# Background work of a scan kernel regrouped into one beat per unit, with read-outs moved and the positive part rebuilt from |s|/2

## The chip, the cores and the metric

One Trainium2 chip, one of its cores. The metric is device time in microseconds (us) of the one launch. Engines are named as in the profile: PE (TensorE: matmuls; PEld its weight loads), DVE (VectorE), ACT (ScalarE), POOL (GpSimd), SP (SyncE, which here only issues DMAs).

## What is computed

Sixteen images of 64 x 64 x 96 in fp32 pass two residual layers, `x = x + L0(gn(x))` and `x = x + L1(gn(x))`, where `gn` is a group norm over 32 groups. Cut to what matters:

```python
def L0(x):      # upsample by FFT, quadratic activation between two 1x1 products, low-pass, take every second
    h = upsample(x) @ W1.T + b1
    h = coef[:, 0] + coef[:, 1] * h + coef[:, 2] * (h * h)
    return lowpass(h @ W2.T + b2)[::2, ::2]

def L1(x):      # a selective scan in four directions
    xc, z = split(x @ in_proj_w.T)
    z = silu(z)
    xc = silu(conv3x3_depthwise(xc) + conv_b)
    xs = stack([rows(xc), columns(xc), reversed rows, reversed columns])     # K = 4, d = 192, L = 4096
    dts, Bs, Cs = split(xs . x_proj_weight)                                   # 6, 16, 16
    delta = softplus(dts . dt_projs_weight + dt_projs_bias)
    # per k, d and state n of 16, along L:
    h[t] = exp(delta[t] * A[n]) * h[t-1] + delta[t] * xs[t] * Bs[t, n]
    y[t] = sum_n h[t, n] * Cs[t, n]   (+ xs * Ds)
    y = layernorm(sum of the four directions) * z
    return y @ out_proj_w.T
```

## The kernel before

**Order.** The program is written out by hand (`manual_schedule`): each engine runs its instructions in exactly the order of the Python calls, and each waits in order. SP issues all DMAs and waits in order too. So what counts is where a call stands among the others of its engine.

**The loop.** `scan` runs 16 images x 8 steps x 6 blocks x 4 units = 3072 units. A step is 1024 positions of one pair of directions; a block is one of six groups of 64 rows (two halves e of 32, each times 4 states on 128 partitions); a unit (n) is one j of four groups of 4 states. `POS = 3 * 8 * 6 * NQ` is the number of slots of an image, three a unit. Per unit:

- POOL makes `b = dtu * bt` for unit n + 2 (`drive`, L827, 128 x 2048), after the odd half's product with ct of unit n (`odd`, L977) in three units of four.
- ACT makes `da = exp(delta * a)` for unit n + 1, one half at a time (`decay`, L821), into PSUM, one buffer a half; and copies the end state of a half (`keep`, L844).
- DVE runs the odd half's scan (`recur(n, 1)`, L836 forwards or L838 backwards), the even half's, then the even half's product with ct (L988). At j = 3 the odd half's product is on DVE too (L968), between the scans.
- PE sums the products over the states (`read_out`, L861, 16 matmul instructions with `fold_s`), in the block's y, with a start from the stored part (L853) in the second pair. `store` copies y (ACT, L872) and writes it out.

Calls of a unit in order: odd scan, odd decay of n + 1, **slot 0**, (odd product and its keep at j = 3), second half of a pending store, odd product on POOL, drive of n + 2, even scan, DVE's keep, **read_out(n - 1)**, **slot 1**, even product, even keep, even decay of n + 1, store of the last block (if unit n - 1 ended one), **slot 2**, fetches.

**Slots.** A slot advances `block_work` and, if due, the background. `block_work` has twelve slots a block (0 to 11: j times 3 plus the slot). In it `task` makes delta and dtu of 128 x 512 for the next use: at slot 0 s = dtw . pr (PE, L683); 1: |s| and exp(-|s|) (ACT); 2: relu(s) and w = 1 + e; 3: ln(1 + e); 4: 1 - w; 6: the sum w + e + ln + relu by four products with the identity (PE, L699) into a new s; 9: dtu = s * u (DVE, L703); 10: delta = s (ACT, L705) and a DMA; 11: the other DMA. In blocks 2 and 3 `mix` (PE, L661) and, in the next block's slot 0, `mixed` (ACT, L666) prepare the next step. All of s and pp share one PSUM bank.

**The background** of image mi is `front(mi + 1)` and after it `finish(mi - 1)`, Python generators that are spread evenly over the slots: a step is due while `n * positions < at * slices`, with 540 slices for front and 117 for finish. In the loop they have two PSUM banks (`b_ps`, bufs 2) and eleven SBUF pieces (L182). `front` has, in order: loads of xt; `norm` (8 sums L205, 8 squares L218 on ACT); the u/h/o part, 4 passes of 3 u groups (L327, copied out at L338) and 5 groups of widen (L278, L285), three h products (L370) with squares (L351), o (L382, copied at L310) and for each second one d (L294, copied at L361, stored by `stow` L303); the e part (L440, L445, put back at L430); a second `norm`; xgp (L459); and the conv part, 12 tiles of 9 taps and z (L487, L499) with two Silu and two table loads on ACT. A step that yields `WAIT` (before the Silus) is only followed at slot 2 of j = 2. `finish` has, for each of 8 tiles: two centred sums yc (L557, L570, ten instructions each), their squares (ACT, L566, L585), yc * z (DVE, L579, L590), the variance v (L586, L591), Ln and Exp (L596, L597), o (L600), DVE's o * r (L606), and the sum e of ob . z0, ob . z1, ident . x1 (L604) and ident . r (L610), copied and written out one step later. For the first image `front(0)` runs alone ahead of the loop, and for the last one `finish(15)` runs alone after it.

Of the kernel before, what the change touches and what calls it, by code (L numbers as in the profile page):

```python
# [70 lines left out]
POS = 3 * 8 * 6 * NQ  # L71
SLICES = 540
FINISH = 117
WAIT = -1


@with_exitstack
def tile_two_blocks(
# [31 lines left out]

    one_s = const.tile([128, 1], F32, name="one_s")
# [14 lines left out]
    ob_s = const.tile([128, 2, C], F32, name="ob_s")  # L126

    with tc.tile_pool(name="setup", bufs=1) as sp, tc.tile_pool(name="setup_ps", bufs=1, space=PSUM) as spp:
# [45 lines left out]
        for i in range(2):  # L174
            nc.vector.tensor_scalar(pd_s[:, i, :], pmat_s[:, i, :], dsum[:, i:i + 1], None, ALU.mult)
            nc.vector.tensor_scalar(ow_s[:, i, :], op_r[:, i, :], on_r[:, i, 0:1], None, ALU.mult)
            nc.vector.tensor_scalar(ob_s[:, i, :], op_r[:, i, :], on_r[:, i, 1:2], None, ALU.mult)

# [3 lines left out]
    b2p = ctx.enter_context(tc.tile_pool(name="b2", bufs=11))  # L182
# [10 lines left out]
    def parts(out, in_, n=4):  # L193

        step = L // n
        for i in range(n):
            nc.sync.dma_start(out=out[:, step * i:step * i + step], in_=in_[:, step * i:step * i + step])  # L197
            yield

    def norm(xt):  # L200

        s = small.tile([C, 8], F32, name="gs")
        for t in range(8):
            junk = piece([C, TB], "junk")
            nc.scalar.activation(junk, xt[:, TB * t:TB * t + TB], AF.Identity, accum_out=s[:, t:t + 1])  # L205
            if t % 2:
                yield
        yield
# [7 lines left out]
        for t in range(8):  # L216
# [4 lines left out]
            if t % 2:  # L221
                yield
        yield
# [10 lines left out]
        yield  # L234
        yield
        return rg, nb

    def front(mi):
# [8 lines left out]
        yield from parts(xt, xc[mi])  # L247
        yield
# [6 lines left out]
        yield  # L255
        yield
# [3 lines left out]
        yield  # L260
# [51 lines left out]
        o_last = None  # L312
        asked = []
        for p0 in range(0, UPS, PP):

            t1 = b18.tile([HW, PP, C], F32, name="t1", tag="b18")
            if not asked:
                asked += [fetch_x(0), fetch_x(1)]
                for _ in range(3):
                    yield  # L320
            for cg in range(3):
                xr = asked.pop(0)
                u_ps = [bank([HW, 16, PP], "u_ps") for _ in range(2)]
                for k in range(16):
                    for a in range(2):
                        on = slice(64 * a, 64 * a + 64)
                        nc.tensor.matmul(  # L327
                            u_ps[a][:, k, :], lhsT=xr[k // 8][on, k % 8, :], rhs=up_s[on, p0:p0 + PP],
                            start=True, stop=True,
                        )  # L330
                    if k == 7:
                        yield
# [3 lines left out]
                for a in range(2):  # L336
                    c0 = 48 * a + 16 * cg
                    nc.scalar.copy(t1[:, :, c0:c0 + 16], u_ps[a].rearrange("w c p -> w p c"))  # L338
                    yield
# [3 lines left out]
            yield  # L343
            for g in range(PP // PG):
                row = p0 + PG * g
                h_ps, hsq = [None] * HB, [None] * HB
                sd = None

                def square(j):
                    hsq[j] = piece([128, PG * UPS], "hsq")  # L350
                    nc.scalar.activation(hsq[j], h_ps[j], AF.Square, bias=b1_s[:, j:j + 1])  # L351

                for j in range(HB + 1):
                    if j == 0 and o_last is not None:
                        keep_o(o_last)
                    elif j == 1 and len(t2) == 2:
                        square(0)
                        d_ps = narrow()
                        yield
                        sd = piece([128, PG * C], "sd")  # L360
                        nc.scalar.copy(sd, d_ps)  # L361
                    elif j:
                        square(j - 1)
                    if j == 2 and sd is not None:
                        stow(sd, row - 2 * PG)
                    if j >= 2 and g == PP // PG - 1 and p0 + PP < UPS:
                        asked.append(fetch_x(j - 2))
                    if j < HB:
                        h_ps[j] = bank([128, PG * UPS], "h_ps")
                        nc.tensor.matmul(  # L370
                            h_ps[j], lhsT=w1t_s[:, 128 * j:128 * (j + 1)],
                            rhs=xu.rearrange("c p q -> c (p q)"), start=True, stop=True,
                        )
                    elif g < PP // PG - 1:
                        xu_ps = widen(t1, g + 1)
                    yield
                o_ps = bank([UPS, PG, C], "o_ps")
                for p in range(PG):
                    if p == 2:
                        yield  # L380
# [5 lines left out]
                    if p == 1 and g < PP // PG - 1:  # L386
                        xu_next = normed(xu_ps)
                o_last = o_ps
                if g < PP // PG - 1:
                    xu = xu_next  # L390
                yield
            if p0 + PP < UPS:
                keep_o(o_last)
                o_last = None
                yield
                if len(t2) == 2:
                    d_ps = narrow()
                    yield
                    sd = piece([128, PG * C], "sd")
                    nc.scalar.copy(sd, d_ps)  # L400
                    yield
                    stow(sd, row - PG)
        keep_o(o_last)
        yield
        d_ps = narrow()
        yield
        sd = piece([128, PG * C], "sd")
        nc.scalar.copy(sd, d_ps)
        yield
        stow(sd, UPS - 2 * PG)  # L410


        def fetch_s(first, n):
            t = b18.tile([UPS, n, C], F32, name="s", tag="b18")
            for k in range(0, n, 8):
                nc.sync.dma_start(out=t[:, k:k + 8, :], in_=s_d[:, first + k:first + k + 8, :])
                yield t, first

        JS = 40
        for _ in range(2):  # L420
            yield
# [700 lines left out]
```

## Time and profile before

| | us |
|---|---|
| median of 3 runs (20474.57 to 20484.85) | 20479.29 |
| the profiled execution: its own time | 20473.08 |
| its span | 20471.3 |
| first drive on POOL (end of `front(0)` and the first tasks) | 468.9 |
| last product on DVE | 20308 |
| tail, `finish(15)` alone | 163 |
| busy: DVE / POOL / PE / ACT | 19208.3 / 19150.8 / 16699.0 / 13815.5 |

A row of the page's fifth part reads: line, engine, operation, output <- inputs, shape, count | busy us, mean ns of one | idle time of the engine just ahead of these instructions, and what ended most of it. In the timeline the idle time ahead of an instruction and its releaser stand in brackets. Neighbouring instructions of DVE and POOL overlap by some 0.07 us in these records, so a chain of them is read from start to start. The page's span does not hold the 1.8 us around the execution.

### The profile page before, as it was taken

The page shows a single profiled execution, that of the slowest core. Times are in us where ns is not written, and L with a number is a line of the kernel's source. Part 1 is how long each engine was busy: PE and PEld are TensorE (multiplying, and loading weights), DVE is VectorE, ACT ScalarE, POOL GpSimd, SP SyncE. Part 2 cuts the span into 40 slices and gives each one's busy share as a digit, 9 for nine tenths or more (in the row PEclk, how much of TensorE's full clock was granted, in tenths as well). Part 3 has the DMA queues.
Part 4 walks back from the last instruction along what each step waited for, and adds up shares of the span by engine and source line. Part 5 has one row for each costly group of instructions (what it writes and reads, how often), then busy time and mean ns, then how long its engine had stood idle before and what let it go on. Part 6 is the DMA issues. An engine that isn't in the chain of part 4 may idle for free. (4 is left out here: it accounts for less than half of the span.)

```text
span 20471.3 us, 274485 instructions
## 1 busy us (share of the span) xinstructions
PE 16699.0 (82%) x98988; PEld 7171.0 (35%) x98988; DVE 19208.3 (94%) x12989; ACT 13815.5 (67%) x20694; POOL 19150.8 (94%) x5384
## 2 busy tenths in 40 slices
PE   7877888888888878788887888888887787888767
PEld 4423334343333433334233343433334333242222
DVE  0999999999999999999999999999999999999997
ACT  4676767667676776766767676676767767677554
POOL 0999999999999999999999999999999999999996
PEclk8888898988889889888888889888898888888888
DMA  2666666766667676666766667667676666766664
GB/s 85 212 224 208 223 234 211 242 214 222 231 218 239 210 240 220 217 235 214 235 218 221 234 215 238 218 220 234 217 237 210 234 223 216 238 217 232 221 214 157
DMA packets 1966064, 4478.55 MB, mean 219 GB/s; under 512 B 461726, under 2 KB 560958, under 8 KB 1962654
## 3 DMA queue, kind: packets, MB, share of 16 engines
q1 hardware_dynamic: 1964702, 4461.00, 64.5%
q8 instruction: 781, 12.80, 0.3%
q14 instruction: 581, 4.76, 0.1%
HBM read 3581.91 MB, written 878.18 MB: 218 GB/s over the span
## 5 line engine op out<-in xcount | busy, mean ns | idle before, releaser
L827 POOL TENSOR_TENSOR b<-dtu,bt 128x2048 f32<-128x2048 f32 x3072 | 13903.4, 4538 | 471.7 <-DMA dtu<-dtu_d 467.9
L821 ACT ACTIVATE da<-delta,a_s 128x1024 f32<-128x1024 f32 x6144 | 6868.4, 1118 | 2264.3 <-DVE b L988 849.7
L977 POOL TENSOR_TENSOR odd<-b,ct 128x1024 f32<-128x1024 f32 x2304 | 5456.2, 2368 | 679.3 <-DVE b L836 246.2
L988 DVE TENSOR_TENSOR b<-da,ct 128x1024 f32<-128x1024 f32 x3072 | 3760.5, 1224 | 41.8
L836 DVE TENSOR_TENSOR_SCAN da<-da,new,b 128x1024 f32<-128x1024 f32 x1440 | 3372.8, 2342 | 82.6 <-ACT da L821 78.9
L838 DVE TENSOR_TENSOR_SCAN da<-da,new,b 128x1024 f32<-128x1024 f32 x1440 | 3370.2, 2340 | 15.8 <-ACT da L821 14.7
L861 PE MATMUL y<-b,fold_s 128*32 128x256 f32 x30720 | 2561.2, 427 | 797.7 <-ACT yt L872 411.5
L844 ACT COPY new<-da 128x1 f32<-128x1 f32 x2880 | 457.1, 159 | 2434.9 <-DVE b L988 1892.3
L836 DVE TENSOR_TENSOR_SCAN b<-da,new,b 128x1024 f32<-128x1024 f32 x864 | 2023.8, 2342 | 29.3 <-ACT da L821 28.3
L838 DVE TENSOR_TENSOR_SCAN b<-da,new,b 128x1024 f32<-128x1024 f32 x864 | 2022.5, 2341 | 29.2 <-ACT da L821 29.2
L487 PE MATMUL c_ps<-xgp,wtap_s 96*64 96x512 f32 (+1 forms) x4608 | 1764.7, 640 | 77.7 <-ACT row L505 71.9
L861 PEld LDWEIGHTS y<-b,fold_s 128*32 128x32 f32 x30720 | 739.7, 114 | 2919.4 <-issue 1557.0
L861 PE MATMUL y<-odd,fold_s 128*32 128x256 f32 x18432 | 1599.9, 421 | 197.3 <-POOL odd L977 197.0
L683 PE MATMUL s<-pr,dtw_s 128*128 128x512 f32 x1536 | 1034.5, 761 | 689.9 <-ACT delta L705 574.0
L661 PE MATMUL pp<-u,xpt_s 128*128 128x512 f32 x1536 | 891.7, 726 | 461.4 <-ACT delta L705 319.1
L699 PE MATMUL s<-w,ident_s 128*128 128x512 f32 x1534 | 1054.0, 775 | 238.4 <-ACT w L694 211.5
L370 PE MATMUL h_ps<-xu,w1t_s 96*128 96x500 f32 x1920 | 1038.8, 642 | 166.1 <-ACT hsq L351 121.1
L836 DVE TENSOR_TENSOR_SCAN da<-da,b 128x1024 f32<-128x1024 f32 x480 | 1096.2, 2284 | 79.2 <-ACT da L821 75.1
L838 DVE TENSOR_TENSOR_SCAN da<-da,b 128x1024 f32<-128x1024 f32 x480 | 1095.2, 2282 | 10.7 <-ACT da L821 9.2
L382 PE MATMUL o_ps<-w2c_s,hsq 128*100 128x96 f32 x9600 | 1009.2, 263 | 71.6 <-ACT hsq L351 71.3
L382 PEld LDWEIGHTS o_ps<-w2c_s,hsq 128*100 128x100 f32 x9600 | 946.0, 176 | 266.2 <-ACT hsq L351 111.4
L487 PEld LDWEIGHTS c_ps<-xgp,wtap_s 96*64 96x64 f32 (+1 forms) x4608 | 631.8, 177 | 1081.2 <-issue 942.6
(140 smaller groups left out, 23002.7 us busy)
## 6 DMA issues: line engine op xcount, KB each, us to landing
dtu<-dtu_d SPq DMA_DIRECT2D x1536, 512.0 KB
delta<-delta_d SPq DMA_DIRECT2D x1536, 512.0 KB
bt<-rows SPq DMA_DIRECT2D x1024, 512.0 KB
ct<-rows SPq DMA_DIRECT2D x1024, 512.0 KB
u<-xs_d SPq DMA_DIRECT2D x1664, 256.0 KB
dtu_d<-dtu SPq DMA_DIRECT2D x767, 256.0 KB
delta_d<-delta SPq DMA_DIRECT2D x767, 256.0 KB
xr<-in_x SPq DMA_DIRECT2D x768, 128.0 KB
```

Source lines behind the costliest of these rows:

```text
L370: nc.tensor.matmul(h_ps[j], lhsT=w1t_s[:, 128 * j:128 * (j + 1)], rhs=xu.rearrange("c p q -> c (p q)"), start=True, stop=True,)
L382: nc.tensor.matmul(o_ps[:, p, :], lhsT=hsq[j][:, UPS * p:UPS * (p + 1)], rhs=w2c_s[:, j, :], start=(j == 0), stop=(j == HB - 1),)
L487: nc.tensor.matmul(c_ps[p:p + n], lhsT=wtap_s[:, tap, 128 * i:128 * i + n], rhs=xgp[:, h0:h0 + 8, dx:dx + HW], start=(tap == 0), stop=(tap ...
L683: nc.tensor.matmul(s, lhsT=dtw_s[:, pair, v, :], rhs=ctx["pr"][t], start=True, stop=True)
L699: nc.tensor.matmul(s, lhsT=ident_s, rhs=of, start=(i == 0), stop=(i == 3))
L821: nc.scalar.activation(da, deltas[n // NQ, e], AF.Exp, scale=a_s[:, k, g, units[n][2]:units[n][2] + 1])
L827: nc.gpsimd.tensor_mul(b, dtus[n // NQ], bt.unsqueeze(1).to_broadcast([128, 2, T]))
L836: nc.vector.tensor_tensor_scan(out, da, b, before, ALU.mult, ALU.add)
L838: nc.vector.tensor_tensor_scan(out[:, ::-1], da[:, ::-1], b[:, ::-1], before, ALU.mult, ALU.add)
L861: nc.tensor.matmul(y[32 * q:32 * q + 32, e, :], lhsT=fold_s, rhs=weighed[e][:, QT * q:QT * q + QT], start=(pair == 0 and j == 0 and e == 0 ...
L977: nc.gpsimd.tensor_mul(odds[n], h, bc[1, r, j])
L988: nc.vector.tensor_mul(bs[n][:, 0, :], h, bc[1, r, j])
```

## The change

It moves and regroups the background; some instructions go.

- **Beats.** The even spread (`POS`, `SLICES`, `FINISH`, `due`) goes. A background advances once per unit, at slot 2; a step that ended in `LIGHT` is also followed at slot 1 and once more at slot 2; one that ended in `VEC` is followed at slot 0 only; `WAIT` stays. front has 176 steps and finish 66 (383 and 114 before); in images 1 to 14 front ends in the image's unit 147 (149 before) and finish in 188 (189 before).
- **Banks.** In `front`, a beat first copies out what the last beat's products left in the two banks (`empty`, the squares, `normed`), then issues new products. `parts` issues its DMAs at once, `stow` and the write of out stand right behind their copies.
- **finish** has per tile, in beats: centre; at slot 0 `rooted` (DVE's o * r and e of the last tile) and loads, at slot 2 square and the last tile's copy out; at slot 0 yz0 and the second centre, at slot 2 its square; at slot 0 yz1 and v, at slot 2 Ln, Exp and o. Every second tile is followed by an empty beat. e is three products, not four: z1 and x1 share one tile zx, x1's last 32 rows stand below r in rx.
- **norm** of the second layer takes its sums from the puts of the e part (`accum_out`), with two tiles in flight.
- **task** starts at slot 11 of the block before; |s| and exp at slot 1, w at 2, ln, 1 - w and the four products at 4, dtu and delta at 9, both DMAs at 10. dtw is halved at the start; s holds s/2, and |s|/2 (`half_s`) is added in the same bank, so Relu and the second s go. mix is at slot 10 and mixed at 11 of the same block.
- **read_out(n)** stands after the even decay of unit n, ahead of slot 2; the store of a block stands in the next unit after the even scan, ahead of slot 1.
- b2 has 12 pieces.

```diff
-    def norm(xt):
+    def norm(xt, s=None):
...
-        s = small.tile([C, 8], F32, name="gs")
-        for t in range(8):
-            junk = piece([C, TB], "junk")
-            nc.scalar.activation(junk, xt[:, TB * t:TB * t + TB], AF.Identity, accum_out=s[:, t:t + 1])
-            if t % 2:
-                yield
-        yield
+        if s is None:
+            s = small.tile([C, 8], F32, name="gs")
+            for t in range(8):
+                junk = piece([C, TB], "junk")
+                nc.scalar.activation(junk, xt[:, TB * t:TB * t + TB], AF.Identity, accum_out=s[:, t:t + 1])
+                if t < 7:
+                    yield LIGHT
...
+        def empty(p0):
+            nonlocal u_ps, o_ps, d_ps
+            if u_ps is not None:
+                for cg, ps in u_ps:
+                    for a in range(2):
+                        c0 = 48 * a + 16 * cg
+                        nc.scalar.copy(t1[:, :, c0:c0 + 16], ps[a].rearrange("w c p -> w p c"))
+            if o_ps is not None:
+                t2.append(piece([UPS, PG, C], "t2"))
+                nc.scalar.copy(t2[-1], o_ps)
+            if d_ps is not None:
+                sd = piece([128, PG * C], "sd")
+                nc.scalar.copy(sd, d_ps)
+                stow(sd, rows.pop(0))
+            u_ps = o_ps = d_ps = None
...
+                empty(p0)
+                grow(0)
+                grow(1)
+                yield
+                square(0)
+                square(1)
+                grow(2)
+                if more:
+                    xu_ps = widen(t1, g + 1)
...
+                yield
+                square(2)
+                if more:
+                    xu = normed(xu_ps)
                 o_ps = bank([UPS, PG, C], "o_ps")
...
+        def rooted(o_ps, r, z0, zx, rx):
+            nc.vector.tensor_mul(rx[0:C], o_ps, r)
+            e_ps = bank([C, TB], "oe_ps")
+            for i, (w, of) in enumerate(((ob_s[:, 0, :], z0), (ob_s[:, 1, :], zx), (ro_s, rx))):
+                nc.tensor.matmul(e_ps, lhsT=w, rhs=of, start=(i == 0), stop=(i == 2))
+            return e_ps
...
+        for t in range(9):
+            yc0 = centre(t, 0, 128) if t < 8 else None
+            yield VEC
+            if left is not None:
+                e_ps = rooted(*left)
...
+                yield
+                sq0 = squared(yc0, 128)
...
+            yield VEC
+            yz0 = scaled(yc0, z0, 128)
+            yc1 = centre(t, 1, 64)
+            yield
+            sq1 = squared(yc1, 64)
+            yield VEC
+            yz1 = scaled(yc1, zx[0:64], 64)
...
-                nc.scalar.activation(m, s, AF.Relu)
...
+                nc.scalar.activation(m, s, AF.Abs, scale=2.0)
+                nc.scalar.activation(e, m, AF.Exp, scale=-1.0)
+                yield
                 nc.scalar.activation(w, e, AF.Identity, bias=one_s)
                 yield
+                yield
                 nc.scalar.activation(d, e, AF.Ln, bias=one_s)
-                yield
                 nc.scalar.activation(w, w, AF.Identity, scale=-1.0, bias=one_s)
-                yield
-                yield
-                s = ps.tile([128, TB], F32, name="s", tag="g")
-                for i, of in enumerate((w, e, d, m)):
-                    nc.tensor.matmul(s, lhsT=ident_s, rhs=of, start=(i == 0), stop=(i == 3))
-                for _ in range(3 - late):
+                for by, of in ((half_s, m), (ident_s, w), (ident_s, e), (ident_s, d)):
+                    nc.tensor.matmul(s, lhsT=by, rhs=of, start=False, stop=(of is d), skip_group_check=True)
+                for _ in range(5):
                     yield
                 dtu, delta = make("dtu"), make("delta")
                 nc.vector.tensor_mul(dtu, s, u)
-                yield
                 nc.scalar.copy(delta, s)
...
+                def at(self, position):
+                    if self.gen is None:
+                        return
+                    if position == 2:
+                        if self.said == LIGHT:
+                            self.step()
+                        if self.gen is not None and self.said != VEC and (self.said != WAIT or j == NQ - 2):
+                            self.step()
+                    elif self.said == (VEC, LIGHT)[position]:
+                        self.step()
...
-                if n >= 1:
-                    read_out(n - 1)
+                if n >= 1 and j == 0:
+                    storing = store(n - 1)
+                    next(storing)
                 slot(1)
...
                 if n < last:
                     decay(n + 1, 0)
-                if n >= 1 and units[n - 1][2] == NQ - 1:
-                    storing = store(n - 1)
-                    next(storing)
+                read_out(n)
                 slot(2)
```

## The prediction

> **What bounds it.** I read the page's first part, then its costliest groups, then the waits of DVE and POOL inside the loop, then the busy time by step of one image, and last a stretch of the timeline. The page:
>
> ```profile
> span 20471.3 us, 274485 instructions
> PE 16699.0 (82%) x98988; PEld 7171.0 (35%) x98988; DVE 19208.3 (94%) x12989; ACT 13815.5 (67%) x20694; POOL 19150.8 (94%) x5384
> ...
> L827 POOL TENSOR_TENSOR b<-dtu,bt 128x2048 f32<-128x2048 f32 x3072 | 13903.4, 4538 | 471.7 <-DMA dtu<-dtu_d 467.9
> ...
> L977 POOL TENSOR_TENSOR odd<-b,ct 128x1024 f32<-128x1024 f32 x2304 | 5456.2, 2368 | 679.3 <-DVE b L836 246.2
> L988 DVE TENSOR_TENSOR b<-da,ct 128x1024 f32<-128x1024 f32 x3072 | 3760.5, 1224 | 41.8
> ```
>
> Two engines are full. POOL has no work for 468 us (the first image's front), and then all but stands still nowhere. Four units (one block) cost POOL four drives, 4.49 us from start to start in the timeline at 10000, and three odd products, 2.31: 24.9 us. DVE in a block, by the same timeline: three units of 5.77 (two scans, 2.26 and 2.24; a copy, 0.13; a product, 1.14) and one of 7.5 with a second product and the dtu product: 24.8. So neither hides the other, and the loop's length is DVE's work plus DVE's idle time. By step, with one image in the middle (image 7) cut at the first scan of each step (columns: length, PE, PEld, DVE, ACT, POOL busy, clock, DMA):
>
> ```profile
> 9466.00:9628.00 162.00, 137.73 (x1028) 75.54 (x1027) 149.62 (x104) 112.27 (x177) 148.83 (x43) 0.86 0.58 195
> 9628.00:9780.30 152.30, 111.14 (x696) 53.22 (x694) 148.66 (x90) 107.08 (x162) 150.43 (x43) 0.82 0.65 222
> ...
> 10083.30:10245.70 162.40, 138.71 (x587) 46.60 (x587) 154.37 (x112) 99.56 (x149) 151.89 (x43) 0.89 0.80 265
> ...
> 19107.80:20300.70 1192.90, 793.53 (x3925) 267.10 (x3924) 1187.67 (x798) 687.11 (x979) 1186.39 (x335) 0.78 0.59 206
> ```
>
> Steps count from 0. DVE and POOL each need 147 to 152 us per step (154 in step 6, which has products of finish on DVE). The lengths differ, up to 162: that is waiting. The last image, with no front behind it, takes 1192.9 / 8 = 149.1 a step. This is the floor. What DVE waits for inside the loop (us, times, longest):
>
> ```profile
> DVE dtu L703 <- PE s L699: 285.7, 224, 3.8
> DVE da L836 <- ACT da L821: 154.0, 149, 3.5
> DVE b L838 <- ACT da L821: 88.2, 73, 2.4
> DVE b L836 <- ACT da L821: 36.5, 45, 1.4
> DVE da L838 <- ACT da L821: 23.9, 47, 0.6
> ```
>
> That is 285.7 for the step sums and 302.6 for decays, 588 of 20471 us: the whole prize inside the loop. One place shows how both come about:
>
> ```profile
> 9479.22 4.07 PE L382 MATMUL o_ps<-w2c_s,hsq 128*100 128x96 f32 x30
> ...
> 9483.12 1.05 PE L699 MATMUL s<-w,ident_s 128*128 128x512 f32 x2
> ...
> 9486.78 0.69 DVE L703 TENSOR_TENSOR dtu<-s,u 128x512 f32<-128x512 f32 x1 [0.80 <-PE s L699]
> ...
> 9487.62 0.68 ACT L351 ACTIVATE hsq<-h_ps,b_s 128x500 f32<-128x500 f32 x1 [3.74 <-PE h_ps L370]
> ...
> 9489.54 2.36 DVE L836 TENSOR_TENSOR_SCAN da<-da,new,b 128x1024 f32<-128x1024 f32 x1 [0.93 <-ACT da L821]
> ```
>
> The four ident products stand behind the background's 30 products on PE; dtu waits 0.80 us. A background square on ACT waits 3.74 us for its bank; the decay behind it is late and the scan waits 0.93.
>
> **Step sums.** Now the ident products are issued at slot 6 of a block's twelve, dtu at slot 9. After: slot 4 and 9, in the same bank, with half|s| added in place of a Relu. So PE has five slots, some 10 us, for 3.6 us of products (9483.12 to 9486.7) and at most one background lump ahead (o_ps 3.2 and d_ps 1.3). Laid out from the end of a block's first scan: DVE takes dtu at 17.3; ACT has w at about 9.9; the sum ends at 12.5 to 15. I take all 285.7 away (bounds -220 to -285.7, the lower if a lump is late now and then). What is late next is POOL, at 24.9 a block. The Relu, 0.59 x 768 = 450 us of ACT, is not on the path, but gives room to decays.
>
> **Decays.** A scan of the even half starts 2.26 us after the even product ends; in that time ACT must copy the end state (0.16, 0.25 after the product) and make the decay (1.12): 0.7 us to spare. The odd decay has 2.4 to spare. The change moves all evacuation behind the even decay, where the spare is the odd decay's. Heaviest usual beat: square and normed, 0.67 + 0.76; the slack holds, with 0.3 us left at slot 4, where Ln and w (1.43) come ahead of the even decay. Where it does not hold: the LIGHT beats (sums, squares, xgp), three a unit, each 0.71 + 0.19. ACT then has per block 9.0 of decays, 0.8 of copies, 4.0 of task, 0.6 of yt and 10.8 of background, 25.2, and in awkward order. They fill some 18 units an image. Today's waits in these places (steps 0 and 4) are about 6.7 us an image, and I leave them. Of the other 200 us half goes: -100 (bounds -250 to +100).
>
> **Banks.** Only two background banks exist in the loop, and a refill now always follows its evacuation in the same beat. In the list of waits PE stands 110.0 us before u_ps and 121.1 before h_ps for ACT to empty a bank; both will grow, by up to 1 us in each of some 150 beats of 15 images, 2200 us of PE. I charge nothing. PE's products in a u/h/o block are some 10.5 us of lumps (u 2.8, h 1.1 each, xu 1.3, o 3.2 and d 1.3 by the rows of the loop), 4 of read-outs, 4.3 of task and 0.9 of mix, 20 out of 24.8, so it has the room; and a lump that starts at 5.8 and lasts 4.4 ends before ACT returns for it at 11.2. If that cover is gone, each lost us comes out as a late bank, then as a late decay (bounds 0 to +230: 0.5 us in each of 31 u/h/o and conv blocks of 15 images). The Trainium skill (Perfetto Trace Analysis, Matmuls) speaks against the change here: groups should rotate through banks, so that one's evacuation overlaps the next one's products; by it the sum would be up to 2200 us higher if PE were the end, and by the rows, where PE waits and nothing waits for it, it stays as it is.
>
> **Read-outs** go half a unit forward on PE, right behind the even product, and the block's store with them. POOL waits behind PE for its odd buffers now (y 68.9, pp 57.4, s 29.3 us), and PE waits for yt (411 and 341 us, by the list of waits). Both shrink, but DVE hardly waits for b (5.4 us), so 0.
>
> **Finish** runs in 42 units before and after (66 beats against 114 slices). But its products for DVE now stand directly behind the odd scan, and each waits for ACT's square, itself behind PE. Take the tile whose centre starts at j=0, from that block's first scan: read-out 3.5 to 4.5, centre 4.5 to 9.0, e_ps 2.6 to 11.6, ident products 8 x 0.43 to 15.0, read-out 16.0, second centre to 20.5, square to 21.1; DVE wants yz1 at 17.9. That is 3.2 us of wait. From j=1, 2 and 3 I get 2.0, 0.3 and 1.3. Two tiles of each: 13.6 us an image; the decays' and squares' shares that are hidden by drift bring it to 10. Fifteen images: +150 (bounds 0 to +400: no wait at all, or one half of a unit per tile). No like wait is in the trace within the loop (0.6 us), so this is the least certain term.
>
> **Ends.** The last image's finish is spread over 188 units now; afterwards it stands in 42, with its waits: +15 (0 to +30). The first front loses the second norm's eight sums (8 x 0.81 us), but two puts come late: -5. The tail's eight tiles each lose two PE products of 0.43: -7. SP now issues xt, x1, ycol in one go; ycol is 3 MB, and in the tail the same took 11.5 us to land, while the next dtu has 14. On SP stow and out now stand directly behind the copies that they store, so SP waits for ACT's beat, and behind it stand the fetches of dtu, delta, bt and ct; these are asked for 11 us or more ahead of use, and SP waits 5134 us for dtu today without harm: 0 for both (to +40).
>
> Sum: -286 - 100 + 150 + 15 - 12 = -233. The profiled execution took 20473.1 (its span and 1.8), 6 us under the median of the runs: 20473 - 233 = **20240 us**, -1.2%.
>
> **Rivals.** (a) Forecast, 20080 to 20420: 0.48. (b) The waits really go: DVE's drop by 500 and finish stays hidden: 20473 - 286 - 230 + 30 = about 19990. For it: blocks in the conv stretch already run at 24.8 with a beat-like order. 0.24. (c) The change only trades waits, within 0.2% (what a measurement of this kernel can tell from no change, some 41 us): finish's waits at about 3 us a tile. 0.08. (d) Slower: the same mechanism beyond its turning point. 120 tiles share out 286 + 100 + 12 - 15 = 383 us, so from 3.2 us of wait per tile on average the change loses. If centre, e_ps and ident products stand in line for a whole unit, 6.2 us a tile, it costs 744: 20830. PE, in order and 95% busy in the last step of this image (149.1 of 157.5), speaks for it; that finish has only 10 of 48 blocks, and that the products are asked a unit apart, speaks against. 0.20.
>
> The range, 19950 to 20620, leaves out the ends of (b) and the worse half of (d). Faster 0.72, same 0.08, slower 0.20.
>
> **What would show it.** DVE's wait for s under 20 us in the loop; decay waits 150 to 250, most of them in steps 0 and 4; steps 1 to 3 at 150 to 152 us each; new waits of yz for sq, about 150 us in all, the largest where the tile starts at j=0; POOL's wait for PE almost gone; a front of some 464 us and a tail of 156. Wrong it is if DVE's wait for decays grows in steps 1 to 3 (the slack at slot 4 is gone), or if yz waits exceed 400.

## The result, and the profile after

The changed kernel takes 20817.57 us (median of 4 runs, 20800.98 to 20818.47), the kernel before 20482.07 beside it: 1.0162 times as long [1.0145, 1.0180]. The forecast was 20240, with a range up to 20620. Its rival (d) named the sign, a wait in finish; that is one of two causes, and the smaller one.

The page of the profiled execution after (20818.47 us, span 20816.7), with the rows that answer to those of before and the row of the product on y0 (the stored part of y, with which a block's read-out begins in the second pair of directions):

```profile
span 20816.7 us, 273741 instructions
...
PE 16622.4 (80%) x98732; PEld 7192.1 (35%) x98732; DVE 19213.7 (92%) x12996; ACT 13446.3 (65%) x19798; POOL 19141.3 (92%) x5384
...
L824 POOL TENSOR_TENSOR b<-dtu,bt 128x2048 f32<-128x2048 f32 x3072 | 13894.7, 4534 | 466.3 <-DMA dtu<-dtu_d 454.7
...
L975 POOL TENSOR_TENSOR odd<-b,ct 128x1024 f32<-128x1024 f32 x2304 | 5438.7, 2361 | 1049.8 <-DVE b L835 562.5
...
L850 PE MATMUL y<-y,ident_s 128*128 128x512 f32 x768 | 550.1, 806 | 752.3 <-DMA y<-part 589.4
```

DVE and POOL do the same work in the same time as before (19213.7 and 19141.3 us busy, 19208.3 and 19150.8 before). The 345 us between the two profiled executions are idle time, but for 5 us of DVE. Image 7 by steps (2, 3, 4, 6 and the last image; columns as before):

```profile
9591.00:9742.70 151.70, 128.88 (x1096) 70.49 (x1096) 148.69 (x103) 104.52 (x164) 149.94 (x43) 0.86 0.67 228
9742.70:9895.40 152.70, 121.69 (x830) 65.62 (x830) 148.16 (x85) 101.32 (x142) 152.45 (x43) 0.90 0.60 205
9895.40:10059.40 164.00, 126.14 (x669) 43.35 (x670) 147.29 (x108) 116.54 (x172) 149.72 (x42) 0.87 0.66 222
...
10214.60:10396.00 181.40, 145.98 (x614) 50.42 (x614) 155.86 (x114) 98.97 (x145) 152.23 (x43) 0.89 0.74 245
...
19435.70:20655.70 1220.00, 787.02 (x3914) 257.99 (x3918) 1190.49 (x798) 674.86 (x935) 1184.83 (x335) 0.78 0.58 201
```

Step 2 fell from 162.0 to 151.7; steps 4 and 6 rose (4 to 7 are the second pair of directions), step 6 from 162.4 to 181.4. Over images 1 to 14, us a block by step, from the starts of the odd scans (the lower rows are runs told below):

| step | 0 | 1 | 2 | 3 | 4 | 5 | 6 | 7 | last image |
|---|---|---|---|---|---|---|---|---|---|
| before | 25.98 | 25.55 | 26.52 | 25.35 | 25.32 | 25.18 | 27.13 | 26.25 | 24.98 |
| after | 25.06 | 24.92 | 25.24 | 25.49 | 27.44 | 25.84 | 30.19 | 27.18 | 25.55 |
| read-outs alone | 25.72 | 26.12 | 25.87 | 25.92 | 25.93 | 26.38 | 27.67 | 27.05 | 25.38 |
| task alone | 25.27 | 25.63 | 25.87 | 25.27 | 25.24 | 24.96 | 26.70 | 26.59 | 24.96 |
| y0 ahead of the beat | 25.10 | 24.91 | 25.13 | 25.49 | 25.49 | 25.07 | 29.11 | 27.00 | 25.52 |
| late first centre | 25.06 | 24.90 | 25.13 | 25.55 | 25.73 | 25.01 | 26.54 | 26.92 | 24.97 |

A difference of 1 in a step is 84 us (14 images, six blocks). Steps 0 to 3 together won 2.69 x 84 = 226 us, steps 4 to 7 lost 6.77 x 84 = 569, the last image 0.57 x 48 = 27: 370 for the loop. Front and tail won 13.2 and 9.6 (first drive at 455.7 us, tail 153.8). With 2 us less for the loop of image 0, which the table leaves out, that is the 345 us. What DVE and PE wait for in the loop after (us, times, longest):

```profile
DVE b L835 <- ACT new L841: 263.4, 101, 9.2
DVE yz L556 <- ACT sq L551: 258.2, 95, 4.7
DVE da L833 <- ACT da L818: 120.4, 68, 4.8
DVE yz L556 <- DMA z<-z_d: 101.5, 26, 6.7
DVE dtu L694 <- PE s L690: 94.7, 59, 4.1
DVE da L835 <- ACT da L818: 70.9, 76, 3.7
```

```profile
PE y L858 <- DVE b L987: 2251.0, 990, 13.3
PE y L850 <- DMA y<-part: 589.4, 165, 9.2
...
PE h_ps L363 <- ACT hsq L370: 94.5, 76, 1.5
...
PE u_ps L345 <- ACT t L326: 38.4, 16, 5.2
```

Three of DVE's waits are new (under 5 us each before): the end state `new` from ACT, the square, and z0. On PE, the wait for y0 was not there before. One place at the end of step 4 shows what it does. The DMA queue first, then PE, ACT and DVE in the timeline:

```profile
10022.48 0.34 SPq L697 DMA_DIRECT2D dtu_d<-dtu  x1
10028.02 0.34 SPq L698 DMA_DIRECT2D delta_d<-delta  x1
...
10031.69 5.81 SPq L512 DMA_DIRECT2D xs_d<-col  x8
10037.60 0.63 SPq L763 DMA_DIRECT2D y<-part  x1
```

```profile
10040.60 2.05 PE L850 MATMUL y<-y,ident_s 128*128 128x512 f32 x2 [7.93 <-DMA y<-part]
...
10051.76 0.69 DVE L694 TENSOR_TENSOR dtu<-s,u 128x512 f32<-128x512 f32 x1 [3.22 <-PE s L690]
...
10052.66 1.99 PE L484 MATMUL c_ps<-xgp,wtap_s 96*128 96x512 f32 x4
...
10054.68 0.69 ACT L500 ACTIVATE row<-c_ps,convb_s 128x512 f32<-128x512 f32 x1 [5.69 <-PE c_ps L484]
...
10057.45 0.59 ACT L695 COPY delta<-s 128x512 f32<-128x512 f32 x1
10057.93 0.17 ACT L841 COPY new<-da 128x1 f32<-128x1 f32 x1
10058.13 1.12 ACT L818 ACTIVATE da<-delta,a_s 128x1024 f32<-128x1024 f32 x1
10059.18 0.15 ACT L841 COPY new<-da 128x1 f32<-128x1 f32 x1
10059.35 2.35 DVE L835 TENSOR_TENSOR_SCAN b<-da,new,b 128x1024 f32<-128x1024 f32 x1 [2.30 <-ACT new L841]
```

The fetch of y0 stands behind eight stores of col on SP, 5.81 us of issuing. PE, which needs y0 half a unit earlier than before, stands 7.93 us. Behind y0 on PE stand the taps of the convolution and the ident products of s: DVE's dtu waits 3.22 us for s, ACT waits 5.69 us for the last taps in a Silu, and behind the Silu stand delta, two end states and the decays. The scan waits 2.30 us.

### The profile page after: what moved, and what is told of

Its sections match the earlier page's. It is cut to its first block, busy times and chain, and to the rows that moved or that the text cites. A ratio compares the mean times of both kernels' runs of the same rounds, so it can differ in the third digit from the quotient of the medians.

```text
span 20816.7 us, 273741 instructions
## 1 busy us (share of the span) xinstructions
PE 16622.4 (80%) x98732; PEld 7192.1 (35%) x98732; DVE 19213.7 (92%) x12996; ACT 13446.3 (65%) x19798; POOL 19141.3 (92%) x5384
## 5 line engine op out<-in xcount | busy, mean ns | idle before, releaser
L858 PE MATMUL y<-b,fold_s 128*32 128x256 f32 x30720 | 2640.4, 439 | 2272.0 <-DVE b L987 2254.9
L835 DVE TENSOR_TENSOR_SCAN da<-da,new,b 128x1024 f32<-128x1024 f32 x1440 | 3371.7, 2341 | 2.7 <-ACT da L818 1.7
L835 DVE TENSOR_TENSOR_SCAN b<-da,new,b 128x1024 f32<-128x1024 f32 x864 | 2023.4, 2342 | 188.4 <-ACT new L841 187.4
L484 PE MATMUL c_ps<-xgp,wtap_s 96*64 96x512 f32 (+1 forms) x4608 | 1688.5, 623 | 5.5 <-ACT xgp L454 5.5
L675 PE MATMUL s<-pr,dtw_s 128*128 128x512 f32 x1536 | 1146.2, 837 | 70.1 <-ACT pr L660 69.9
L835 DVE TENSOR_TENSOR_SCAN da<-da,b 128x1024 f32<-128x1024 f32 x480 | 1095.8, 2283 | 71.5 <-ACT da L818 69.2
L363 PE MATMUL h_ps<-xu,w1t_s 96*128 96x500 f32 x1920 | 1044.6, 656 | 137.8 <-ACT hsq L370 94.5
L850 PE MATMUL y<-y,ident_s 128*128 128x512 f32 x768 | 550.1, 806 | 752.3 <-DMA y<-part 589.4
L390 PE MATMUL o_ps<-w2c_s,hsq 128*100 128x96 f32 x9600 | 1069.2, 277 | 101.1 <-ACT hsq L370 100.8
L690 PE MATMUL s<-w,ident_s 128*128 128x512 f32 x1534 | 941.5, 700 | 244.0 <-ACT w L688 241.0
L390 PEld LDWEIGHTS o_ps<-w2c_s,hsq 128*100 128x100 f32 x9600 | 1027.2, 191 | 271.1 <-ACT hsq L370 162.8
L690 PE MATMUL s<-m,half_s 128*128 128x512 f32 x1534 | 1005.4, 742 | 1.0 <-ACT m L681 1.0
```

Source lines behind the costliest of these rows:

```text
L363: nc.tensor.matmul(h_ps[j], lhsT=w1t_s[:, 128 * j:128 * (j + 1)], rhs=xu.rearrange("c p q -> c (p q)"), start=True, stop=True,)
L390: nc.tensor.matmul(o_ps[:, p, :], lhsT=hsq[j][:, UPS * p:UPS * (p + 1)], rhs=w2c_s[:, j, :], start=(j == 0), stop=(j == HB - 1),)
L484: nc.tensor.matmul(c_ps[p:p + n], lhsT=wtap_s[:, tap, 128 * i:128 * i + n], rhs=xgp[:, h0:h0 + 8, dx:dx + HW], start=(tap == 0), stop=(tap ...
L675: nc.tensor.matmul(s, lhsT=dtw_s[:, pair, v, :], rhs=ctx["pr"][t], start=True, stop=False, skip_group_check=True)
L690: nc.tensor.matmul(s, lhsT=by, rhs=of, start=False, stop=(of is d), skip_group_check=True)
L835: nc.vector.tensor_tensor_scan(out[:, ::-1], da[:, ::-1], b[:, ::-1], before, ALU.mult, ALU.add)
```

## The experiments

**Theories.** P: PE's wait for y0 makes the losses in steps 4 and 5 and part of 6. F: finish's products, directly behind the odd scan, wait for their squares. Rivals: the read-outs themselves block PE; late loads of delta, ycol and z0; the order of the copies on ACT. All ratios are to the kernel before, run beside each kernel; intervals in brackets. Each quoted text says what its own letters stand for.

### Parts alone in the kernel before

**Task alone** (slots, half|s|, mix and mixed as after; beats, read-outs and finish as before):

```diff
-                s = ps.tile([128, TB], F32, name="s", tag="g")
-                for i, of in enumerate((w, e, d, m)):
-                    nc.tensor.matmul(s, lhsT=ident_s, rhs=of, start=(i == 0), stop=(i == 3))
+                for by, of in ((half_s, m), (ident_s, w), (ident_s, e), (ident_s, d)):
+                    nc.tensor.matmul(s, lhsT=by, rhs=of, start=False, stop=(of is d), skip_group_check=True)
```

> The kernel before with the task part of the change alone (half magnitudes in one bank, products at slot 4, dtu and delta at 9, mix at 10 and mixed at 11); read-outs, front and finish as before. By the prediction's first step DVE's 286 us of waiting for the sums go: about 20200 to 20260. Rival: the sums stand behind the uneven background lumps all the same and dtu waits stay above 100 us, or ACT's decays take the place of the waits: 20350 to 20480.

Measured: 20312.29, ratio 0.9918 [0.9903, 0.9932]. DVE's waits in the loop:

```profile
DVE da L842 <- ACT da L827: 225.4, 171, 4.4
DVE b L844 <- ACT new L850: 55.8, 15, 4.0
DVE yz L593 <- ACT sq L588: 52.4, 25, 2.5
...
DVE dtu L703 <- PE s L699: 18.3, 30, 6.7
```

The wait for s goes as forecast. But new waits of 55.8 and 52.4 come up elsewhere, so the net gain is 168 us (0.0082 x 20480) and not 286. The time lies between the two texts, under the rival's range and over the forecast.

**Read-outs and store alone** (the rest as before):

```diff
-                if n >= 1:
-                    read_out(n - 1)
+                if n >= 1 and j == 0:
+                    storing = store(n - 1)
+                    next(storing)
                 slot(1)
...
+                read_out(n)
                 slot(2)
```

> The kernel before with the read-outs and the store moved as in the change, and nothing else (y0 fetched at the end of j = 3, as before). By theory P the move alone makes PE wait for y0 in the second pair, some 500 us of PE in all, and steps 4 to 7 longer by 0.5 to 1.5 us a block: 20550 to 20800, while steps 0 to 3 (first pair, no y0) do not get longer. If the wait for y0 needs the beats as well (bulk of DMAs in one slot ahead of it on SP): within 40 us of 20481.

Measured: 20795.41, 1.0154 [1.0139, 1.0169], without any wait of PE for y0. The waits of PE (first line) and DVE:

```profile
PE y L861 <- DVE b L989: 3202.0, 1213, 11.7
```

```profile
DVE dtu L703 <- PE s L699: 343.1, 257, 9.5
DVE da L838 <- ACT da L821: 249.3, 231, 2.6
DVE da L836 <- ACT da L821: 246.9, 231, 2.9
```

PE, in order, stands 3202 us for the even product (276 before) with the background's products behind it. With the old even spread ACT then waits for those banks ahead of a decay; one place in the timeline:

```profile
9524.72 0.77 ACT L285 ACTIVATE xu<-xu_ps,nb,rg 96x500 f32<-96x500 f32 x1 [4.00 <-PE xu_ps L278]
...
9525.57 1.12 ACT L821 ACTIVATE da<-delta,a_s 128x1024 f32<-128x1024 f32 x1
9526.72 2.36 DVE L836 TENSOR_TENSOR_SCAN da<-da,new,b 128x1024 f32<-128x1024 f32 x1 [1.20 <-ACT da L821]
```

ACT waits 4.00 us for xu_ps, and the scan 1.20 for the decay behind it. Steps 1 and 3 to 7 get slower. The time falls into the range of theory P (20550 to 20800) by luck: its wait for y0 is not there, and the first pair gets slower in two of its steps. So moved read-outs are not free by themselves. In the changed kernel PE stands for it too (2251 us), and steps 0 to 3 run at 24.9 to 25.5 all the same. There the emptying stands behind the even decay; that this order is what absorbs the wait is argued from the two, not shown by a run of its own.

### The stored part y0

**y0 one unit early** (after, fetched at the end of j = 2), and **y0 ahead of slot 2** and **ahead of slot 1** of the last unit:

```diff
-                if j == NQ - 1 and n < last and steps[units[n + 1][0]][1] == 1:
-                    st2, bi2, _ = units[n + 1]
+                if j == NQ - 2 and n + 2 <= last and steps[units[n + 2][0]][1] == 1:
+                    st2, bi2, _ = units[n + 2]
```

> The changed kernel, with the stored part y0 of the next block fetched one unit earlier (at the end of j = 2 instead of j = 3). Theory P (read-outs): in the second pair a block's read-out begins with a PE product on y0; since it moved half a unit forward it stands on PE before y0 has landed (589 us of PE waiting for that DMA), everything behind it on PE is late, above all the conv products c_ps and z_ps, so the Silus, the keep and the odd decay behind them, and the scan of j = 0 (263 us). Then steps 4 and 5 fall from 27.0 and 26.7 us a block to about 25.3 and 25.0, and the time to about 20560 (-260). Theory D (delta): the odd decay is late because the copy of delta now stands between the Silus and it; then y0 is beside the point and the time stays at 20800 or above.

Measured: 20495.04, 1.0009 [1.0000, 1.0018], under theory P's 20560; PE's wait for y0 and the wait for s are gone, the wait for `new` falls from 266 to 88 us.

> The kernel after with one edit: y0 for the next block is fetched in the last unit ahead of slot 2 (ahead of that beat's loads and stores on SP), not behind it; SP's wait for the copy of delta (the stores at slot 10) stays ahead of it. Theory B (the bulk of the beat delays y0): PE's wait for y0 falls from 589 to under 150 us, the time to 20500 to 20600. Rival W (SP's wait for ACT's copy of delta delays y0, the bulk adds little): PE's wait stays above 350 us, the time 20700 to 20800.

Measured: 20478.45, 0.9999 [0.9990, 1.0009]. Of PE's wait this is left:

```profile
PE y L850 <- DMA y<-part: 65.1, 14, 5.5
```

> The same with y0 fetched ahead of slot 1 of the last unit, so in front of the stores of dtu and delta too. Both theories let PE's wait for y0 end (under 30 us): the time is that of the run with y0 fetched one unit early, 20480 to 20530. How far it lies under the run with y0 ahead of slot 2 is what SP's wait for delta costs: under 60 us by theory B, 200 us or more by rival W.

Measured: 20493.95, 1.0006 [0.9997, 1.0016]. The three agree within their intervals. One fetch moved past one slot's DMAs wins back 334 us ((1.0162 - 0.9999) x 20480). SP's wait for the copy of delta, which stands ahead of both (10022.48 to 10028.02 above), adds nothing that can be measured. Theory P holds, and the bulk of the beat is its cause. It takes the early read-outs too: without the beats there was no such wait (read-outs alone), and with the beats and late read-outs a third of it is left (next run).

**Read-outs back** (after, with `read_out(n - 1)` and the store in their old places):

> The changed kernel with the read-outs and the store back in their old places (read-out of unit n - 1 ahead of slot 1 of unit n, the store behind the even decay). Theory P: PE's wait for y0 goes with them, steps 4 and 5 fall as in the run with y0 early, and steps 0 to 3 stay near 25.0 a block; about 20550 to 20650. Theory D: about 20800. If the read-outs are what made steps 0 to 3 fast, these rise to 25.5 or more and the gain is eaten.

Measured: 20557.88, 1.0041 [1.0026, 1.0056], as theory P has it. The waits of PE:

```profile
PE y L850 <- ACT yt L869: 425.2, 103, 10.0
...
PE y L858 <- ACT yt L869: 284.1, 61, 6.5
PE h_ps L363 <- ACT hsq L370: 272.9, 90, 4.9
...
PE y L850 <- DMA y<-part: 186.7, 39, 9.4
```

This hides most of y0 (187 us are left of 589), but PE waits 709 us for yt again. The wait for the bank h_ps, 94.5 us in the changed kernel, is 272.9 here. With y0 in time the early read-outs are the better ones, by 0.3 to 0.4%.

**Copy of delta back at slot 10** (after):

```diff
                 nc.vector.tensor_mul(dtu, s, u)
-                nc.scalar.copy(delta, s)
                 yield
+                nc.scalar.copy(delta, s)
```

> The kernel after with one edit: the copy of delta is issued at slot 10 of a block again, one slot behind dtu, as before. Theory Q (the late Silus and decays come from PE standing for y0, so the order on ACT behind it does not matter): 20780 to 20840. Rival D (the copy of delta, put behind late Silus and ahead of the odd decay, is what makes the scan of j = 0 wait): the wait of R1 for ACT's new (266 us) falls under 100, the time to about 20550 to 20650.

Measured: 21007.17, 1.0257 [1.0242, 1.0272]. (R1 in the text is the odd half's scan.) Both texts fail. s and pp share a bank, and PE's mix now waits for the copy:

```profile
PE pp L655 <- ACT delta L696: 325.9, 144, 5.0
```

That wait is 37.3 us in the changed kernel; in the kernel before, PE waited 574 and 319 us for the same copy, a fact of the waits that the forecast passed over.

### Loads and the places of finish

**ycol in six parts**, three a unit (after):

```diff
-        parts(ycol[0], y_d[1, 0:128, :])
-        parts(ycol[1], y_d[1, 128:DI, :], 2)
+        for to, src, k in ((ycol[0], y_d[1, 0:128, :], 4), (ycol[1], y_d[1, 128:DI, :], 2)):
+            for i in range(k):
...
+                yield LIGHT
```

> The changed kernel with the six loads of ycol (3 MB) spread over two units instead of one beat. Theory L: the bulk stands ahead of the next block's delta on SP and on the DMA engines; ACT's decay waits for delta (279 us in all, once an image for some 7 us on average) and DVE for it, about 5.6 us in the block behind; spread, 60 to 95 us go: about 20730. If delta is late for another reason: no change.

Measured: 20821.48, 1.0170 [1.0154, 1.0185]. The wait for `new` falls from 266 to 156 us, those for the square and z0 rise from 258 and 101 to 306 and 173: moved, not removed. Step 6 falls to 27.91 us a block and step 7 rises to 29.79.

**VEC at slot 1** (after; finish's products behind the even scan instead of the odd one):

```diff
-                    elif self.said == (VEC, LIGHT)[position]:
+                    elif position == 1 and self.said in (VEC, LIGHT):
```

> The changed kernel with VEC steps followed at slot 1 instead of slot 0, so that finish's products on DVE stand behind the even scan, some 2.4 us later, and their PE work with them. Theory F (finish waits on its squares): DVE's wait of yz for sq inside the loop, about 315 us, falls to 50 to 120, steps 6 and 7 by about 1.5 us a block, time about 20600. Rival L (finish is late on its loads): what waits is the load queue, z0 101 us and delta 279 us; the waits only move and the time stays within 50 us of 20817.

Measured: 20672.72, 1.0097 [1.0080, 1.0113]; yz's wait for its square falls from 258 to 78 us, as theory F has it, but steps 6 and 7 only by 0.7 and 0.2 us a block, not 1.5.

**Old finish** (after with y0 early; finish as before, spread over its 117 slices):

> The changed kernel with y0 fetched early and finish as it was before (114 slices, spread evenly over the slots of what is left of the image). If the remaining excess over the prediction's front part is finish alone, steps 6 and 7 fall from 29.2 and 27.0 us a block to about 27 and 26.2 and the last image from 25.56 to 25.0: 20495 - 15 x 6 x 3.0 - 28 = about 20200. If the beats of front are at fault as well, 20350 or more.

Measured: 20318.50, 0.9920 [0.9906, 0.9935], 182 us under the same kernel with finish in beats, and between the two texts. Here PE stands 6.4 to 10.4 us in each of images 1 to 14 for the first tile's y (114 us in all; in the kernel before 64), and block 2 of step 6 (counted from 0) takes 33.3 us.

**Tiles from j = 1** and **from j = 0** (after with y0 early; every tile starts in the same unit of a block, four units a tile):

```diff
-            yield
-            if t % 2:
-                yield
+            yield FIRST
```

> The kernel after with the fetch of y0 at the end of j = 2, and every tile of finish started (its first centre) at slot 2 of j = 1, four units a tile, without the empty beat. Theory F (the wait of yz for its square depends on the j at which the tile starts; with y0 early the tiles cost 2.8 to 3.8 us from j = 0, about 0.2 from j = 1, 2.1 to 2.7 from j = 2): the wait of yz for sq falls from 185 to under 50 us, the time from 20495 to about 20300 to 20350. Rival L (in the second pair the loads decide: delta and z0 are late behind the bulk on SP, and a tile that waits less for its square waits for z0 instead): the waits of yz together stay above 200 us and the time within 40 us of 20495.

> The same as the run with tiles from j = 1, but every tile starts at slot 2 of j = 0. Theory F: 120 tiles at 2.8 to 3.8 us, so the wait of yz for sq is 330 to 450 us, the time 20600 to 20750, some 300 above the run with tiles from j = 1. Rival L: within 60 us of that run.

Measured: 20451.62, 0.9986 [0.9977, 0.9995] from j = 1, and 20599.62, 1.0057 [1.0042, 1.0072] from j = 0. The wait of yz for sq, j = 1 first:

```profile
DVE yz L557 <- ACT sq L552: 141.9, 107, 4.2
```

```profile
DVE yz L557 <- ACT sq L552: 277.0, 101, 4.7
```

The unit in which a tile starts is worth 0.7% of the time, some 150 us: F is right in kind, but it said 300. The first run fell short of its forecast: 141.9 us and not under 50. With 102 us of waiting for z0 beside it, it is nearly what rival L says (over 200 us for yz; 43 us under 20495, where L allows 40), while the second run speaks against L. By tile (means over images 1 to 14), from j = 0 the second product waits 2.8 to 3.8 us in five of eight; from j = 1 it waits 0.1 to 0.6 in six, and 3.3 in two, whose square stands behind mix. One of these in the timeline:

```profile
10315.15 2.02 PE L543 MATMUL yc<-ycol,pmat_s 128*64 128x512 f32 x4
...
10317.10 2.84 PE L655 MATMUL pp<-u,xpt_s 128*128 128x512 f32 x6
...
10319.98 0.69 ACT L660 ACTIVATE pr<-pp,bumps_s 128x512 f32<-128x512 f32 x1 [2.97 <-PE pp L655]
...
10320.57 0.58 ACT L552 ACTIVATE sq<-yc 64x512 f32<-64x512 f32 x1
...
10321.18 0.68 DVE L557 TENSOR_TENSOR yz<-yc,zx 64x512 f32<-64x512 f32 x1 [3.06 <-ACT sq L552]
```

yc is complete at 10317.2; ACT, in order, waits 2.97 us for mix's products first and squares afterwards. So the price of a tile is set by what stands ahead of its square, on PE or on ACT. Note that yz takes nothing from sq: both only read yc, yet yz waits till sq has read. The Trainium skill (PSUM — Partial Sum Buffer, PSUM bank collisions raise a hardware error) says that two engines may not touch one bank of the same partitions at once, two readers included; the 3.06 us are in line with that, and no run here took the order away.

### Versions put together

**Four mends** (after with y0 early, VEC at slot 1, ycol in parts, z0 loaded a tile ahead):

> The changed kernel with y0 fetched early, VEC steps at slot 1, ycol's loads spread over two units, and z0 loaded a beat earlier (with the next tile's y0, u0 and yu). If finish's waits are those of its order and its loads (theories F and L together), the 185 us of yz for sq and 89 us of yz for z0 that stayed with y0 early mostly go: about 20495 - 180 = 20310. If they only move to other waits of finish, as in the run with ycol spread alone, 20420 to 20500.

Measured: 20351.85, 0.9938 [0.9921, 0.9955], between the two texts.

**Tiles from j = 1 with the loads mended** (y0, z0 and ycol):

> The run with tiles from j = 1, and in addition z0 loaded with the other loads of its tile and the 3 MB of ycol issued in six parts. Theory F and the loads both: yz waits for sq and z0 together under 60 us, dtu 0, decays 200 to 230 in all: 20150 to 20250, under all kernels so far. Rival L2 (the parts of ycol only move the wait, as they did in the kernel after): no better than the run with tiles from j = 1.

Measured: 20375.88, 0.9949 [0.9932, 0.9965]. The waits for z0 and `new` go (102 and 89 us to 0 and 22), and the wait for the square rises from 142 to 254: it seems that a late load had covered part of it. The forecast of 20150 to 20250 was too low, and rival L2 fails too: the loads are worth 76 us.

**Late first centre** (the kernel with the old finish and four more empty steps ahead of its first centre):

```diff
         ahead = fetch_y(0)
-        for _ in range(2):
+        for _ in range(6):
...
-                    if self.gen is not None and self.n * self.positions < self.slots * 117:
+                    if self.gen is not None and self.n * self.positions < self.slots * 121:
```

> The kernel with the old finish, evenly spread, and the early y0 (20318), with four more empty steps ahead of the first centre. There PE waited 135 us in all for the first tile's load of y (up to 7.8 us an image), and block 2 of step 6 took 33.3 us. If that load is the rest: block 2 of step 6 at 28 to 29, the time 20240 to 20280, under all kernels so far. Rival: the decay of that block is late for another reason, the time within 30 us of 20318.

Measured: 20228.63, 0.9874 [0.9859, 0.9889], the fastest of all. Block 2 of step 6 falls from 33.3 to 28.3 us, and PE's wait for the first tile's y from 114 to 8 us. DVE's waits:

```profile
DVE da L840 <- ACT da L823: 161.5, 135, 4.8
DVE da L838 <- ACT da L823: 111.6, 66, 3.9
DVE yz L589 <- ACT sq L584: 32.6, 14, 2.3
```

## Why the prediction was wrong

The forecast's sum was -233 us, the measured difference of the profiled executions +345, 578 more. The runs split it, each against the kernel before. What finish in beats costs depends on the old finish that it is compared with, the one as before (0.9920) or the one with a late first centre (0.9874), and the first row with it:

| | forecast | measured | from |
|---|---|---|---|
| task, beats of front, banks, read-outs, ends | -398 | -164 to -258 | old finish: 0.9920; late first centre: 0.9874 |
| finish in beats, and its last image | +165 | +182 to +276 | y0 one unit early, less these: 1.0009 - 0.9920 and 1.0009 - 0.9874 |
| y0 behind the beat's DMAs | 0 (to +40) | +313 | after, less y0 one unit early: 1.0162 - 1.0009 |
| sum | -233 | +331 | 1.0162 - 1 |

The columns add up (331 by the ratios, 345 by the profiled executions). DVE's waits in the loop, in us, show the same:

| | scans for decays | scans for `new` | dtu for s | yz for squares | yz for z0 |
|---|---|---|---|---|---|
| before | 302.6 | 0 | 285.7 | 0.6 | 4.7 |
| after | 211.0 | 265.8 | 94.7 | 258.2 | 101.5 |
| y0 ahead of the beat | 219.5 | 88.6 | 0 | 179.5 | 72.8 |
| late first centre | 292.8 | 13.5 | 0 | 34.3 | 0 |

- **Failed: the step on SP in Ends** ("SP now issues xt, x1, ycol in one go ... 0 for both (to +40)") together with **Read-outs** ("so 0"). It listed the fetches that stand behind the beat (dtu, delta, bt, ct) and how long ahead they are asked for, and left out y0, which PE needs sooner after its fetch than before; and it looked at what the read-outs let go earlier, not at what they need earlier. The wait measured 589 us on PE and cost 313 to 334 us by the three y0 runs.
- **Failed too, by less: Decays.** -100 was forecast. In the changed kernel the wait for decays falls to 211, but the scans' wait for ACT's end states, which stand beside the decays on ACT, is new and larger. With y0 in time the two together are 308 to 334 us in the three y0 runs, with the late first centre 306: nothing was won.
- **Right: Step sums.** The wait for s falls to 18.3 us with the task alone, and to 0 with y0 early. But with the task alone 118 of the 286 us are lost to other waits.
- **Right in kind, too small: Finish.** +150 in the loop was forecast; the beats with the last image cost 182 to 276, and with y0 early yz waits 290 us. The bounds held. The layout by j did not: j = 0 costs what was worked out (3.2 forecast, 2.8 to 3.8 measured), and j = 1 less (0.1 to 0.6, not 2.0), but 3.3 where the square stands behind mix, which the layout left out. With y0 early, tiles from j = 2 wait 2.0 to 2.6 us for the first product's square (0.3 forecast), and those from j = 3 wait 2.2 and 5.2 us (1.3 forecast), mostly for the load of z0, which the layout left out as well.
- **Right in time, not in its reason: Banks.** Steps 0 to 3 took 24.9 to 25.5 us a block. The text had PE's waits for emptied banks grow at no charge; they shrank (h_ps from 121.1 to 94.5, u_ps from 110.0 to 38.4). With the read-outs back in their old places they are 272.9 and 109.5. So it seems that the early read-outs, at which PE stands 2251 us for the even product, take the place of these waits. The Trainium skill (Perfetto Trace Analysis, Matmuls) asks for rotating banks, so that emptying one overlaps filling the next; here the two are emptied and refilled in one beat, and no run here rotates more of them.
- **Right: front and tail in Ends.** They won 13 and 10 us (12 forecast).
- **Of the signs named:** decay waits of 150 to 250 came true in number (211), though nothing was won by it; s under 20 and POOL's wait for PE almost gone did not (94.7; y 126.2, pp 30.3, s 23.3), the first because of y0; yz waits for sq were 258. Neither sign of being wrong came: yz waits 360 us with z0, not over 400, and the waits for decays in steps 1 to 3 fell from 107 to 97 us. The signs watched only waits that the sum had thought of, and not y0.

Left open: why the early read-outs cost 1.5% in the kernel before and nothing with the beats was read from two traces and not taken apart; and the best version with finish in beats (0.9938) stays 0.6% above the evenly spread one (0.9874), so whether beats can be placed to cost finish nothing is not known.

## What to carry to other kernels

When a consumer is moved forward, list everything it reads, and for each the queue that brings it, with what the same change puts ahead on that queue; the one with the least time to spare decides, and moving that one DMA past the bulk may be the whole cure. A wait on an engine that is idle anyway is free only if nothing in order behind it feeds the bound engine: ask it for each instruction behind the wait. Removed waits come back in part at the next late thing, so here the gain read off a list of waits was an upper bound.

## What the runs showed beside this

- Issuing is not free on SP: eight DMAs of col take 5.81 us to issue (0.7 each), while a store of dtu takes 0.34.
- A scan that starts from a constant is shorter than one that starts from a state: in the changed kernel 480 scans of `da<-da,b` (L835) average 2283 ns, 1440 of `da<-da,new,b` 2341. Blocks of the first step of a direction, where no state exists yet, take 24.3 us where nothing waits, and not 24.8.
- Taking away a late load can leave the time where it was, because the wait beside it grows by as much (ycol in parts: 266 to 156 us for `new`, 360 to 479 for square and z0).
